# Indirect gathers of a graph kernel's second product handed out from a queue, with pauses that read fresh values

## The chip, the cores and the metric

The kernel runs on one core of one Trainium2 chip. The time is device microseconds of one execution; the number to predict is the median over runs of the changed kernel. A trace of one profiled execution shows every instruction of the engines: TensorE (PE; its weight loads are PEld), VectorE (DVE), ScalarE (ACT), GpSimd (POOL) and SyncE (SP), and the DMA queues.

## The reference

Four graph layers run on the same 4096 nodes with 128 features, each with a residual and a layer norm. `adj` is a 4096 x 4096 matrix with about two entries per thousand outside its diagonal.

```python
x = _layernorm(x + L0(x, adj))     # signed attention over adj
x = _layernorm(x + L1(x, adj))     # Chebyshev, K = 3, twice
x = _layernorm(x + L2(x, adj))     # 4-head attention over adj.T
x = _layernorm(x + L3(x, adj))     # degree-normalised mean

def cheb_conv(x, L, W, b):         # L1 applies it twice, with elu
    Tx0 = x
    out = Tx0 @ W[0]
    Tx1 = L @ x
    out = out + Tx1 @ W[1]
    for k in range(2, W.shape[0]):
        Tx2 = 2.0 * (L @ Tx1) - Tx0
        out = out + Tx2 @ W[k]
        Tx0, Tx1 = (Tx1, Tx2)
    return out + b
```

So layer 1 multiplies `adj` four times: by x (product 1 below), by t1 = adj x (product 2), by v (product 3) and by w (product 4).

## The kernel before

The nodes are cut into 8 blocks of 512 (`IB`), each block into 4 tiles of 128. A chunk is one 512 x 512 piece of `adj`, 1 MB, brought in by SyncE. `propagate` (line 723) multiplies a stationary operand by one block row of chunks, 8 chunks a block, and after each chunk calls `seen`, which carries the side work of that moment. A call of `seen` is a hook; its number counts chunks within the product.

Some blocks are not multiplied densely at all. `adj` is sparse, so VectorE finds the entries of each row (`take`, lines 1402 and 1403: the eight largest of a row and where they are), and `Lists.build` (from line 1411; its instructions all show as line 1318) makes a list of neighbours for each block. A block that is in `LAST` (0 and 1, left out of product 2) or `PAIRED` (0, 1 and 2, left out of product 3) is then computed from gathered rows: `rows_of` gathers for each tile, called a unit, 9 times 128 rows by an index list; `weigh` (lines 1557 to 1562) scales them on ScalarE and VectorE; `product` (lines 1631 to 1640 in product 2, 1688 to 1708 in product 3) sums them on TensorE. The entries of `adj` themselves are gathered by `pairs`, 36 gathers a block, and taken over by `paired` (lines 1545 to 1547, on VectorE).

Every such gather goes through `by_index` (line 1524): an indirect DMA issued by GpSimd, followed by `pause` (line 1569), a 128 x 1 multiplication on GpSimd. A pause can be given a value to read; without one it reads a constant of its own.

Four things set the order of the work. First, within products 1 to 3 a planner orders each engine's instructions by priority and its own estimates. Second, what is passed to `tc.keep_in_program_order` keeps its order on its engine; that holds for all gathers and their pauses on GpSimd. Third, `chained` ties VectorE's instructions together in the order in which the program writes them: `take`, `paired`, `build`, `weigh`, the block's t2T (line 779) and the copy of w (line 826) in products 2 and 3. Fourth, product 4 and all that follows runs in an order written out by hand, with 3 gathers a hook.

Product 2 works on blocks 2 to 7, so its hooks run from 0 to 47. After a block, `second_end` (line 781) makes hT from three products (line 786), two elu (VectorE's part is line 721), two more products (line 791) and v (ScalarE's copy, line 793), and v goes to DRAM for the gathers of product 3. Units 0 to 7 belong to the blocks 0 and 1; their gathers land in parts of hT, t1T and xT that are free at that time. The last of their products, unit 3 and unit 7, call `second_end` for the blocks 0 and 1. Which hook does what stands in `plan`: units are pulled at hooks 0, 0, 12, 13, 25, 25, 35 and 37, the pairs of block 1 are fetched at 7, those of block 2 at 26 (12 of them) and at 45 (the rest).

Product 3 works on blocks 3 to 7 (hooks 0 to 39). It weighs 12 units, at hooks 6, 9, 11, 14 and so on, and pulls unit u + 2 in the product of unit u, into three buffers. It also builds the lists of blocks 3 to 7. Product 4 is in `sparse_layers`; after it the gathers for layer 2 begin (`early`, then `gathers`, line 1846).

Of the kernel before, what the change touches and what calls it, by code (L numbers as in the profile page):

```python
# [21 lines left out]
P = 128  # L22
IB = 512
TB = IB // P
# [15 lines left out]
PAIRED = [0, 1, 2]  # L40
# [7 lines left out]
def adj_resnorm_d4(ctx: ExitStack, tc: tile.TileContext, x_in, xT_in, adj, adjT, pairs, diag_in, w0g, w0gT, a0, w1a, b1a,  # L48
# [633 lines left out]
    def network(usual):  # L682

        with ExitStack() as whole:
# [3 lines left out]
            with ExitStack() as first, ExitStack() as l1h_pool:  # L688
# [15 lines left out]
                if usual:  # L704
                    lists = Lists(whole, first, l1h_pool, own_entries)
# [44 lines left out]
                pairs = {c: lists.pairs(c) for c in PAIRED} if usual else {}  # L750

                def fetch(c, n):
                    for _ in range(n):
                        next(pairs[c], None)

                made = lists.build(0) if usual else None
                done = []
# [18 lines left out]
                v = state.tile([P, NT, F], F32, name="v")  # L776
# [4 lines left out]
                def second_end(ib, t2T):  # L781
                    blk = slice(ib * IB, (ib + 1) * IB)
                    for hh in range(HH):
                        ph = ps_mm.tile([P, IB], F32, name="pmm")
                        for k, r in enumerate((xT[:, blk], t1T[:, blk], t2T)):
                            nc.tensor.matmul(ph, W1A[:, k, hh * P:(hh + 1) * P], r, start=k == 0, stop=k == 2)
                        elu(hT[:, hh, blk], ph, B1A[:, hh:hh + 1], B1N[:, hh:hh + 1])
                    q = ps_tr.tile([P, TB, F], F32, name="ptr")
                    for k in range(TB):
                        for hh in range(HH):  # L790
                            nc.tensor.matmul(q[:, k, :], hT[:, hh, (ib * TB + k) * P:(ib * TB + k + 1) * P],
                                             w2x[:, hh, :], start=hh == 0, stop=hh == HH - 1)
                    nc.scalar.copy(v[:, ib * TB:(ib + 1) * TB, :], q)
                    done[-1] = ib
                    if usual:
                        lists.store(0, ib, v)

                second = second_product(lists, l1w, pairs, t1, t1T, xT, hT, v, done, t2_of, second_end) if usual else None

                for ib, blk, p in propagate(lambda jt: t1[:, jt, :], order=[0, 4, 1, 5, 2, 6, 3, 7], seen=second, blocks=[b for b in range(NB) if not usual or b not in LAST]):  # L800
                    t2T = l1w.tile([P, IB], F32, name="t2T")
                    r = t2_of(t2T, p, blk)
# [5 lines left out]
                w = state.tile([P, NT, F], F32, name="w", tag="yn")  # L808
# [1 line left out]

                third = None
                if usual:
                    fetch(PAIRED[-1], TB * 9)
                    lists.paired(PAIRED[-1])
                    l1s = l1h_pool.enter_context(tc.tile_pool(name="l1s", bufs=2, reuse_waits="tile"))
                    third = third_product(lists, l1s, ps_tr, ps_mm, v, w, hT, W1B, wd, h0T)
# [5 lines left out]
                for ib, blk, p in propagate(lambda jt: v[:, jt, :], beside=times_w1, seen=third, blocks=[b for b in range(NB) if not usual or b not in PAIRED]):  # L822
                    lvT = l1w.tile([P, IB], F32, name="t2T")
                    nc.scalar.copy(lvT, p)
                    q = transpose4(ps_tr, "ptr", lambda k: lvT[:, k * P:(k + 1) * P])
                    r = nc.vector.tensor_copy(w[:, ib * TB:(ib + 1) * TB, :], q)
                    if usual:
                        lists.chained(r)
                        lists.store(1, ib, w)
                    ph = ps_mm.tile([P, IB], F32, name="pmm")  # L830
                    for hh in range(HH):
                        nc.tensor.matmul(ph, wd[:, hh, :], hT[:, hh, blk], start=hh == 0, stop=hh == HH - 1)
                    nc.scalar.copy(h0T[:, blk], ph)
# [337 lines left out]
            with tc.manual_schedule(engines={mybir.EngineType.PE, mybir.EngineType.DVE, mybir.EngineType.Activation,  # L1171
# [126 lines left out]
                this, nt, _, tau2 = behind.popleft()  # L1298
# [21 lines left out]
    class Lists:  # L1320
# [3 lines left out]
        def __init__(self, whole, first, layer, own_entries):  # L1324
# [9 lines left out]
            self.at = keep.tile([P, NT - TB, NB, 8], U16, name="at")  # L1334
            self.diag = own_entries
            self.last = None
            nc.scalar.dma_start(self.diag, diag_in)
            self.source = keep.tile([P, NT, NEAR + QT], I32, name="source")
            self.value = keep.tile([P, NT, NEAR + QT], F32, name="value")
            self.where = keep.tile([P, NT, QT], I32, name="where")  # L1340
            units = len(PAIRED) * TB
# [13 lines left out]
            with tc.tile_pool(name="lists_i", bufs=1) as pool:  # L1355
                i = pool.tile([P, SLOTS], I32, name="i")
                for t, pattern, base, step in ((self.slot, [[1, SLOTS]], 0, 0), (self.place, [[0, TB], [P, QT]], 0, 1),
                                               (self.first, [[IB, NB], [0, 8]], 1, 0), (self.own, [[0, 1]], 0, 1)):
                    n = flat(t).shape[1]
# [162 lines left out]

        def by_index(self, out, of, index):
            tc.keep_in_program_order(nc.gpsimd.indirect_dma_start(out, None, of, bass.IndirectOffsetOnAxis(ap=index, axis=0)))  # L1524
            tc.keep_in_program_order(self.pause())

        def values(self, c):
            flat = adjT.rearrange("a b p k i -> (a b p k i)")[:, None]
# [76 lines left out]
    def second_product(lists, pool, pairs, t1, t1T, xT, hT, v, done, t2_of, second_end):  # L1605
        units = len(LAST) * TB
        E = NEAR + QT
        late = slice(5 * IB, 8 * IB)
        soon = slice(2 * IB, 5 * IB)
        places = [t[:, cols].rearrange("p (j f) -> p j f", f=F)  # L1610
                  for t, cols in ((hT[:, 0], late), (hT[:, 1], late), (t1T, soon), (xT, soon))]
        got = places[0:2] * 2 + places[2:4] * 2
        made, sums = {}, {}
        plan = {}

        def at(h, f, *args):
            plan.setdefault(h, []).append(lambda: f(*args))

        def fetch(c, n):
            for _ in range(n):  # L1620
                next(pairs[c], None)

        def pull(u):
            deque(lists.rows_of(u, got[u], 2), 0)

        def weigh(u):
            here = pool.tile([P, F], F32, name="here2", bufs=1)
            lists.weigh(u, t1[:, tile_of(u), :], got[u], here, got[u][:, E:E + QT, :], True)
            made[u] = here

        def product(u):
            t, k = tile_of(u), u % TB
            if k == 0:
                sums[0] = pool.tile([P, IB], F32, name="t2T")
            p = lists.psum.tile([P, P], F32, name="u")
            nc.tensor.matmul(p, made.pop(u), ident, start=True, stop=False)
            for j in range(QT):
                nc.tensor.matmul(p, got[u][:, j, :], got[u][:, E + j, :], start=False, stop=j == QT - 1)
            t2_of(sums[0][:, k * P:(k + 1) * P], p, slice(t * P, (t + 1) * P))
            if k == TB - 1:  # L1640
                second_end(PAIRED[u // TB], sums.pop(0))

        for c, h in ((1, 0), (2, 14)):
            build = lists.build(c, True)
            for n in range(3):
                at(h + 3 * n, next, build)
        at(0, pull, 0)
        at(0, pull, 1)
        at(7, fetch, 1, TB * E)
        at(8, lists.paired, 0)  # L1650
        at(26, lists.paired, 1)
        for u, h in enumerate((9, 11, 27, 30, 33, 35, 41, 44)):
            at(h, weigh, u)
            at(h + 1, product, u)
        for u, h in ((2, 12), (3, 13), (4, 25), (5, 25), (6, 35), (7, 37)):
            at(h, pull, u)
        at(26, fetch, 2, 12)
        at(45, fetch, 2, TB * E)
        hooks = [0]

        def seen(ib, n, c, a):
            h = hooks[0]
            hooks[0] += 1
            if c in FAR:
                lists.take(ib, c, a, True)
            for f in plan.pop(h, ()):
                f()
            if h == 47:
                assert not plan and not made and not sums
        return seen  # L1670
# [63 lines left out]
    def sparse_layers(enter, lists, w, h0T):  # L1734
# [4 lines left out]
        E = NEAR + QT  # L1739
        W = 3 * H + 1  # L1740
        ld = ld_of[0]
        rows = state.tile([P, NT, F + H], F32, name="rows", tag="v")
# [93 lines left out]
        got, told, wide = {}, {}, {}  # L1836
# [172 lines left out]
        with tc.manual_schedule(engines={mybir.EngineType.PE, mybir.EngineType.DVE, mybir.EngineType.Activation,  # L2009
# [22 lines left out]
            def pull():  # L2032
                for u in range(len(LAST) * TB):
                    pulled[u] = l2.tile([P, E, F + H], F32, name="got", bufs=4)
                    yield from lists.rows_of(u, pulled[u], 1)
                for c in (4, 5, 6, 7):
                    yield from lists.values(c)
# [7 lines left out]
            def product(u):  # L2045
                c, k = PAIRED[u // TB], u % TB
                if k == 0:
                    apart[c] = ps_p.tile([P, IB], F32, name="pp")
                p = apart[c][:, k * P:(k + 1) * P]
                here, into = weighed.pop(u)  # L2050
                g = pulled.pop(u)
                nc.tensor.matmul(p, here[:, 0:F], ident, start=True, stop=False)
                for j in range(QT):
                    nc.tensor.matmul(p, g[:, j, 0:F], into[:, j, :], start=False, stop=j == QT - 1)
                if k == TB - 1:
                    end = block_end(c, apart.pop(c))
                    next(end)
                    others.append(end)

            plan = {}  # L2060
            for u, h in enumerate((7, 10, 13, 16, 19, 22, 25, 28)):
                plan.setdefault(h, []).append(lambda u=u: weigh(u))
                plan.setdefault(h + 1, []).append(lambda u=u: product(u))
            pulls = pull()
            known = None
            load_spread(0)
            order = [0, 1, 3, 4, 5, 6, 2, 7]
            hook = 0
# [119 lines left out]
```

## Time and profile before

| what | value |
|---|---|
| median of 13 runs | 1638.67 us (1635.86 to 1640.21) |
| the profiled execution | 1641.54 us, its span 1639.7 us |
| mean granted TensorE clock | 0.952 |
| busy: TensorE, VectorE, GpSimd, ScalarE | 1473.6, 1139.7, 839.1, 387.4 us |
| share of the chain that ended last: PE, DVE, DMA, POOL | 46%, 28%, 8%, 7% |
| product 2, from its first to its last chunk product | 564.2 to 800.9 us |
| first chunk product of product 3, of product 4 | 804.2, 1003.1 us |
| both_ways gathers (pairs) | 108, median 974 ns |
| pauses that read the constant | 508, median 205 ns |

A row of a timeline gives start and duration in us, engine, line, operation, the tiles written and read, shapes and count; square brackets hold the idle time of the engine just before, with what ended it. Idle time of an engine that nobody waits for costs nothing, and shares over the whole span mix stages with different limits.

### The profile page before, as it was taken

The numbers are of one execution on the slowest core, as the hardware profiler recorded it, in microseconds if no ns is written. First come the engines' busy times: TensorE is split into PE (matmuls) and PEld (weight loads), VectorE is DVE, ScalarE is ACT, GpSimd is POOL, SyncE is SP. The second block draws the span as 40 slices with busy tenths as digits, with TensorE's granted clock in tenths as the row PEclk, the third lists the DMA queues.
The fourth block names the chain that finished last, engine by engine and source line by source line (L and its number), as shares of the span: only waits on it lengthen the run. The fifth ranks groups of instructions, "written<-read, shape, count | busy, mean of one in ns | idle before, by whom it ended". The sixth has DMA issues, their size and how long they took to land.

```text
span 1639.7 us, 16500 instructions
## 1 busy us (share of the span) xinstructions
PE 1473.6 (90%) x4740; PEld 711.6 (43%) x4744; DVE 1139.7 (70%) x3209; ACT 387.4 (24%) x698; POOL 839.1 (51%) x1336
## 2 busy tenths in 40 slices
PE   6899999999999999999999999999916798789885
PEld 3344444544444444444444454545413344444344
DVE  5987655788978887998699971455326756556766
ACT  5775540010000011121200000222313111122234
POOL 0000000000243088848485888888886688888841
PEclk9999999999999999999999999999966788889988
DMA  9867776479798885867587889998874577678773
GB/s 381 340 258 298 256 258 247 169 265 316 298 324 309 308 290 176 296 213 273 171 302 260 263 275 318 315 303 296 258 176 134 178 242 244 224 240 282 233 191 102
DMA packets 111199, 421.47 MB, mean 257 GB/s; under 512 B 21685, under 2 KB 48314, under 8 KB 71290
## 3 DMA queue, kind: packets, MB, share of 16 engines
q1 hardware_dynamic: 59984, 360.01, 61.4%
q0 software_dynamic: 22656, 36.17, 8.9%
q10 hardware_dynamic: 28458, 24.14, 5.1%
q8 instruction: 39, 0.64, 0.2%
q14 instruction: 62, 0.51, 0.1%
HBM read 404.39 MB, written 15.86 MB: 256 GB/s over the span
## 4 chain that ended last, share of the span: by engine, by line
PE 46%; DVE 28%; DMA 8%; POOL 7%; issue 6%; ACT 3%; ACTq 0%; DVEq 0%; POOLq 0%; SPq 0%
PE pacc L731 12%; PE pacc L424 12%; PE pp L2076 7%; DVE at L1403 5%; PE pp L1957 5%; DVE top L1402 4%; DMA got<-table,source 4%; POOL got L1846 3%; DVE gw L1882 2%; DMA chunk<-in_adjT 2%; DVE acc L1970 2%; POOL got L1524 1%; DVE here L1884 1%; DVE here L1562 1%; POOL idle L1569 1%
## 5 line engine op out<-in xcount | busy, mean ns | idle before, releaser
L1846 POOL DMA_INDIRECT got<-table,source x267 | 255.5, 957 | 64.0 <-issue 57.1
L1957 PE MATMUL pp<-chunk,xT 128*128 128x512 f32 x496 | 245.0, 636 | 1.3 <-ACT xT L1928 0.7
L731 PE MATMUL pacc<-chunk,x 128*128 128x512 f32 x512 | 223.1, 593 | 1.0 <-DMA chunk<-in_adjT 1.0
L1524 POOL DMA_INDIRECT got<-rows,source x180 | 183.7, 1021 | 67.4 <-issue 37.6
L424 PE MATMUL pacc<-chunk,hw 128*128 128x512 f32 x408 | 188.6, 607 | 0.8 <-DVE hw L467 0.7
L1360 POOL IOTA i<- 128x384 int32 (+3 forms) x4 | 0.9, 237 | 346.6 <-PE pden L412 329.2
L731 PE MATMUL pacc<-chunk,t 128*128 128x512 f32 x384 | 171.5, 597 | 0.0
L2076 PE MATMUL pp<-chunk,w 128*128 128x512 f32 x384 | 170.2, 592 | 0.0
L731 PEld LDWEIGHTS pacc<-chunk,x 128*128 128x128 f32 x512 | 95.9, 190 | 116.3 <-issue 113.7
L731 PE MATMUL pacc<-chunk,v 128*128 128x512 f32 x320 | 144.5, 597 | 0.0
L1402 DVE MAX8 top<-chunk 128x8 f32<-128x512 f32 x196 | 128.6, 678 | 14.9 <-DMA chunk<-in_adjT 14.9
L1957 PEld LDWEIGHTS pp<-chunk,xT 128*128 128x128 f32 x496 | 94.9, 204 | 91.9 <-issue 85.8
L1403 DVE FIND_INDEX8 at<-top,chunk 128x8 uint16<-128x512 f32 x196 | 133.1, 685 | 0.0
L1569 POOL TENSOR_TENSOR idle<-idle 128x1 f32<-128x1 f32 x508 | 115.7, 228 | 8.9
L1524 POOL DMA_INDIRECT both_ways<-in_pairs,both_at x108 | 106.8, 989 | 17.4 <-issue 17.0
L424 PEld LDWEIGHTS pacc<-chunk,hw 128*128 128x128 f32 x408 | 75.0, 192 | 91.9 <-issue 86.2
L731 PEld LDWEIGHTS pacc<-chunk,t 128*128 128x128 f32 x384 | 71.7, 192 | 81.8 <-issue 81.8
L396 ACT ACTIVATE junk<-chunk 128x2048 fp8e4<-128x2048 f32 x51 | 97.4, 1909 | 28.5 <-DMA chunk<-in_adjT 27.9
L2076 PEld LDWEIGHTS pp<-chunk,w 128*128 128x128 f32 x384 | 70.5, 190 | 77.3 <-issue 76.5
L330 DVE TENSOR_SCALAR pos<-chunk 128x2048 bf16<-128x2048 f32 x66 | 80.2, 1221 | 33.7 <-DMA chunk<-in_adjT 33.6
L1889 PE MATMUL u<-gw,into 128*128 128x132 f32 x192 | 33.7, 320 | 70.5 <-DVE gw L1882 70.5
L731 PEld LDWEIGHTS pacc<-chunk,v 128*128 128x128 f32 x320 | 58.3, 190 | 65.5 <-issue 65.5
(433 smaller groups left out, 2063.3 us busy)
## 6 DMA issues: line engine op xcount, KB each, us to landing
chunk<-in_adjT SPq DMA_DIRECT2D x326, 1024.0 KB
keep<-in_adjT SPq DMA_DIRECT2D x13, 1024.0 KB
spread<-spread ACTq DMA_DIRECT2D x16, 384.0 KB
got<-table,source POOLq DMA_INDIRECT x267
chunk<-in_adjT ACTq DMA_DIRECT2D x4, 1024.0 KB
got<-rows,source POOLq DMA_INDIRECT x180
table<-rows ACTq DMA_DIRECT2D x8, 264.0 KB
xT<-in_xT ACTq DMA_DIRECT2D x8, 256.0 KB
```

The lines of the kernel that those rows point to most:

```text
L330: r = nc.vector.tensor_scalar(pos, a, 0.0, None, op0=ALU.is_gt)
L396: nc.scalar.activation(junk, a, AF.Relu, scale=-1.0, accum_out=bad[:, n:n + 1], saturate=False)
L424: in_order(nc.tensor.matmul(p, hw[:, j * TB + k, :], a[:, k, :], start=first and k == 0, stop=last and k == TB - 1))
L731: nc.tensor.matmul(p, stationary(c * TB + k), a[:, k, :], start=n == 0 and k == 0, stop=n == NB - 1 and k == TB - 1)
L1402: pin(nc.vector.max(self.top[:, t, ib, :], row))
L1403: pin(nc.vector.max_index(self.at[:, t - TB, ib, :], self.top[:, t, ib, :], row))
L1524: tc.keep_in_program_order(nc.gpsimd.indirect_dma_start(out, None, of, bass.IndirectOffsetOnAxis(ap=index, axis=0)))
L1569: return nc.gpsimd.tensor_tensor(self.idle[:, 0:1], of, self.idle[:, 1:2], ALU.mult)
L1846: nc.gpsimd.indirect_dma_start(got[t][:, j, :], None, table, bass.IndirectOffsetOnAxis(ap=lists.source[:, t, j:j + 1], axis=0))
L1889: nc.tensor.matmul(so, into[:, j, :], gw[:, j, :], start=j == 0, stop=False)
L1957: nc.tensor.matmul(p, y[:, t0 + k, :], a[:, ib % (TB // n), k, :], start=k == 0, stop=k == n - 1)
L2076: nc.tensor.matmul(p, w[:, c * TB + k, :], a[:, k, :], start=n == 0 and k == 0, stop=n == NB - 1 and k == TB - 1)
```

## The change

Only units and pairs of product 2 are concerned by the queue; the pauses of all gathers that go through `by_index` are.

- `ask` puts a generator of gathers in a queue, with the hook from which it may be handed out. `feed`, called at the end of every hook of product 2, adds 3.4 to a credit, hands out one gather for each whole unit of it, in the queue's order, and keeps at most 3.4. `finish` hands out everything up to and including one generator, or everything that is left.
- The pulls and fetches of product 2 are asked for in place of being issued at once: units at hooks 2, 2, 12, 14, 25, 25, 35 and 37, pairs at 7, 26 and 45. `weigh` and `paired` call `finish` for what they need. What is left after product 2 is handed out before `paired` of block 2.
- `by_index` gives its pause `lists.fresh` to read: a column of the newest v, of the newest t2T of a unit, or of the newest w, as the program has written them so far. It starts as None and is set to None again after product 3.

```diff
-                    done[-1] = ib
                     if usual:
+                        lists.fresh = v[:, ib * TB, 0:1]
                         lists.store(0, ib, v)
...
-                    fetch(PAIRED[-1], TB * 9)
+                    lists.finish()
                     lists.paired(PAIRED[-1])
...
                         lists.chained(r)
+                        lists.fresh = w[:, ib * TB, 0:1]
                         lists.store(1, ib, w)
...
+            self.fresh = None
+            self.queue, self.credit = deque(), 0.0
...
-            tc.keep_in_program_order(self.pause())
+            tc.keep_in_program_order(self.pause(self.fresh))
+
+        def ask(self, hook, rows):
+            self.queue.append((hook, rows))
+            return rows
+
+        def feed(self, hook, rate):
+            self.credit += rate
+            while self.credit >= 1 and self.queue and self.queue[0][0] <= hook:
+                if next(self.queue[0][1], self) is self:
+                    self.queue.popleft()
+                else:
+                    self.credit -= 1
+            self.credit = min(self.credit, rate)
+
+        def finish(self, rows=None):
+            while self.queue and any(rows is None or r is rows for _, r in self.queue):
+                deque(self.queue.popleft()[1], 0)
...
-        def pull(u):
-            deque(lists.rows_of(u, got[u], 2), 0)
+        rows = [lists.rows_of(u, got[u], 2) for u in range(units)]
+
+        def some(c, n):
+            for _ in range(n):
+                if next(pairs[c], pairs) is pairs:
+                    return
+                yield
 
         def weigh(u):
+            lists.finish(rows[u])
...
             t2_of(sums[0][:, k * P:(k + 1) * P], p, slice(t * P, (t + 1) * P))
+            lists.fresh = sums[0][:, k * P:k * P + 1]
             if k == TB - 1:
                 second_end(PAIRED[u // TB], sums.pop(0))
...
-        at(0, pull, 0)
-        at(0, pull, 1)
-        at(7, fetch, 1, TB * E)
+        def known(c):
+            lists.finish(asked[c])
+            lists.paired(c)
+
+        asked = {}
+        for h, what in ((2, 0), (2, 1), (7, (1, TB * E)), (12, 2), (14, 3), (25, 4), (25, 5), (26, (2, 12)), (35, 6), (37, 7), (45, (2, TB * E))):
+            if isinstance(what, int):
+                lists.ask(h, rows[what])
+            else:
+                asked[what[0]] = lists.ask(h, some(*what))
         at(8, lists.paired, 0)
-        at(26, lists.paired, 1)
+        at(26, known, 1)
...
-        for u, h in ((2, 12), (3, 13), (4, 25), (5, 25), (6, 35), (7, 37)):
-            at(h, pull, u)
-        at(26, fetch, 2, 12)
-        at(45, fetch, 2, TB * E)
...
             for f in plan.pop(h, ()):
                 f()
+            lists.feed(h, 3.4)
...
+            lists.finish()
+            lists.fresh = None
             pulls = pull()
```

## The prediction

> **What bounds the kernel now.** I read the page first (engine shares, then the 40 slices), then a table of busy time by stage, then the order of time on GpSimd, VectorE, ScalarE and TensorE around product 2, product 3 and the start of the sparse layers. The table of stages comes first here; its columns are stretch, length, busy time of each engine with instructions in brackets, granted clock, DMA share, GB/s.
>
> ```profile
> 564.00:620.00 56.00, 55.30 (x167) 26.27 (x166) 50.98 (x135) 6.94 (x11) 39.27 (x64) 1.00 0.84 290
> 764.00:804.00 40.00, 39.52 (x126) 19.98 (x125) 24.90 (x61) 7.69 (x14) 28.40 (x47) 1.00 0.60 198
> 804.00:884.00 80.00, 74.36 (x226) 33.59 (x225) 72.58 (x264) 8.18 (x15) 48.32 (x72) 1.00 0.77 274
> 884.00:967.00 83.00, 78.23 (x267) 38.57 (x266) 77.26 (x282) 6.03 (x13) 68.73 (x106) 1.00 0.79 266
> 1003.00:1100.00 97.00, 93.54 (x286) 46.65 (x286) 38.62 (x130) 17.56 (x33) 83.50 (x147) 1.00 0.93 315
> 1201.00:1235.00 34.00, 0.40 (x8) 0.31 (x6) 6.45 (x24) 5.16 (x10) 27.84 (x44) 0.50 0.78 181
> ```
>
> Product 2 (564 to 804) keeps TensorE full. That hides what sets the end, which the last row shows: TensorE does 0.40 us in 34 us there. Who is late then is on the timelines of TensorE and GpSimd:
>
> ```profile
> 1187.87 1.26 POOL L1569 TENSOR_TENSOR idle<-rows,idle 128x1 f32<-128x1 f32 x5
> 1189.84 0.97 POOL L1524 DMA_INDIRECT got<-table_early,source  x1 [0.71 <-issue]
> 1219.42 0.97 POOL L1846 DMA_INDIRECT got<-table,source  x1 [0.15 <-issue]
> 1234.84 1.69 PE L1889 MATMUL u<-gw,into 128*128 128x132 f32 x6 [33.60 <-DVE gw L1882]
> ```
>
> GpSimd gathers with gaps of 0.15 us, and TensorE waits for the last of those gathers. Five pauses stand back to back just before: GpSimd was behind all through the first sparse product. Going back, its gaps stay below 1.2 us as far as 888.61. So GpSimd is a solid line from 888.61 to 1234, and what starts it late there, ends everything late. What starts it at 888.61 is the weighing of unit 1 on VectorE:
>
> ```profile
> 805.32 0.18 DVE L1546 COPY value<-both_ways 128x36 f32<-128x36 f32 x1
> 805.56 0.29 DVE L1318 TENSOR_SCALAR there<-top 128x256 f32<-128x256 f32 x1
> 818.21 0.16 DVE L1318 COPY base<-u 128x4 f32<-128x4 f32 x1 [1.84 <-PE u L1454]
> 884.82 0.85 DVE L1559 TENSOR_SCALAR hot<-iota,into_column,back 128x128 f32<-128x128 f32 x3
> 885.22 1.00 PE L1694 MATMUL ptr<-got,hot 128*128 128x128 f32 x6
> 888.61 0.97 POOL L1524 DMA_INDIRECT got<-rows,source  x1 [12.54 <-issue]
> ```
>
> VectorE is one chained order from `paired(2)` (805.32) through three list builds to 884.82; the only wait printed there is 1.84 us. So the path is: `paired(2)` on VectorE, 80 us of list building, product of unit 1, GpSimd's 346 us of gathers, the sparse layers.
>
> **The change, part by part.** *Queue arithmetic.* I counted `feed` by hand (3.4 a hook, what is left over capped at 3.4). All units and the pairs of block 1 are handed out before their `finish` would force them. The 24 last pairs of block 2, asked for at hook 45, come as 6, 4 and 3 at hooks 45 to 47, and 11 in `finish()` after product 2. Before, all 24 ran without a wait up to 796.1 (last line below).
>
> *What the pauses read there.* At hook 45 `product(7)` runs first and calls `second_end(1)`, so the pauses of the first 13 read v of block 1. The other 11 read v of block 7, whose `second_end` follows hook 47. These are the two ScalarE copies (first two lines), and the GpSimd rows for the pace:
>
> ```profile
> 796.66 0.59 ACT L793 COPY v<-ptr 128x512 f32<-128x512 f32 x1 [1.52 <-PE ptr L791]
> 814.74 0.59 ACT L793 COPY v<-ptr 128x512 f32<-128x512 f32 x1 [2.98 <-PE ptr L791]
> ...
> 793.76 0.97 POOL L1524 DMA_INDIRECT both_ways<-in_pairs,both_at  x1 [0.15 <-issue]
> 795.11 0.97 POOL L1524 DMA_INDIRECT both_ways<-in_pairs,both_at  x1 [0.15 <-issue]
> ```
>
> One gather with its pause takes 795.11 - 793.76 = 1.35 us. Gather 1 of the 24 runs at about 763; its pause waits until 797.25 (796.66 + 0.59), and behind it on GpSimd stand the other 23, then units 0 and 1 of product 3 and all later gathers; `paired(2)` waits for the 24. Gather 2 starts at 797.6, twelve take 16.2, so gather 14 starts at 813.8; its pause waits until 815.33. Gathers 15 to 24 start from 815.7; the last at 815.7 + 9 x 1.35 = 827.9.
>
> *Landing.* The chain shows 2.34 us from the start of a gather to its reader in one place (1229.84) and 5.08 in another (971.40). So `paired(2)` reads at 830.2 to 833.0; I take 831.5, nearer the lower end, since 1 KB is little. The Trainium skill, "DMA: Bandwidth & Descriptors", section on the anatomy of a SWDGE DMA, gives about 2.0 us fixed for each such DMA; counted from the end of the issue, that would be 830.9, which agrees.
>
> *VectorE.* L1546 moves from 805.32 to 831.5: 26.2 us later, and everything chained waits behind it: builds 3 to 7, all weighing, the copies of w. In the meantime VectorE can do only the two unchained L721 of block 7 (0.6 us each, 1.2 in all), perhaps saving the 1.84 wait too. Shift of the chained order: 23.2 to 25.0, I take 24.5. No wait between 805 and 885 takes it up, so the product of unit 1 comes at 909.7 and GpSimd's unit 4 starts at 913.1.
>
> *GpSimd at the start of product 3.* Its first gather moves from 818.67 to 829.2, 10.6 us; that lies inside the 12.54 us before 888.61 and costs nothing by itself.
>
> *Pauses in product 3.* They read v of block 7, then w of the block just ended. Only one is late beside its gather: unit 6 starts at 914.83, its first gather ends at 915.94, and it reads w of block 4,
>
> ```profile
> 914.83 1.11 POOL L1524 DMA_INDIRECT got<-rows,source  x1 [0.15 <-issue]
> ...
> 919.61 0.68 DVE L826 COPY w<-ptr 128x512 f32<-128x512 f32 x1
> ```
>
> done at 920.2. Both are 24.5 later, so the wait is about 4.3 us, and GpSimd has no slack. Unit 3 waits some 9 us for w of block 3 (872.47), but then it waits for the product of unit 1 anyway. Unit 9 (955.90, w of block 5 at 959.09) is already 4.3 late: nothing. From below the term is 0, from above 4.3 for each of units 6 and 9, 8.6.
>
> *Earlier waits in product 2.* The pairs of block 1 and units 2 and 3 end at 679.5 instead of 676; weighing of unit 2 is at 700.9. Units 4 and 5 wait for v of block 4 (about 693.3) and end at 716; they are weighed at 726.2 and 735.2. Units 6 and 7 were held by the products of 4 and 5 before, too. Cost nothing, hidden by those 10 to 20 us. A pause reads 128x1 as before: 0.20 us. The removed `done[-1] = ib` is Python alone.
>
> *What could be gained.* TensorE waits 7.8 us in all for VectorE in product 2. Its rows name t2T, hT and here, none behind a gather; gain from 0 to 7.8, I take 0, as TensorE's end of product 2 starts nothing that is late.
>
> *A rule weighed.* Gathers last 0.97 us beside VectorE's searches in product 2 (above) and 1.24 us beside the list builds (823 to 829). The Trainium skill, "SBUF — State Buffer", on the trap in which VectorE blocks a DMA, says that descriptor writing is shut out while certain VectorE instructions run. By that rule the 10 gathers from 815.7 would save 10 x 0.27 = 2.7 us, as VectorE stands still; I have counted them at the undisturbed 1.35 already.
>
> **Sum.** 24.5 + 4.3 = 28.8 us, against the profiled execution's 1641.54: 1670.3. That execution lies 2.9 above the median of 1638.67, so I say 1667.5. TensorE starts the first sparse product later as well, by some 14 to 22 us, less than GpSimd, so it doesn't add. From 1235 on the order is unchanged; a clock other than the 0.87 there by 0.01 would move TensorE's 327 busy us by 3.8.
>
> **Rivals.** (a) *Not slower.* The pauses pace gathers alongside TensorE, the 7.8 us of TensorE's waits in product 2 go, and the late `paired(2)` finds slack: 1638.7 - 7.8 = 1631. It decides if 26 us of waiting that ends elsewhere lies between 805 and 1234 on VectorE or GpSimd; I find 1.84 and about 12.5, the latter being VectorE's own lateness. Chance 0.05. (b) *VectorE is not held.* If builds come before `paired(2)` in VectorE's real order, only GpSimd's start (hidden) and the 4.3 remain: 1643. Against it: in the trace L1546 stands directly before build 3, and both are chained. Or the planner takes up half of the shift: 1653. Together 0.11. (c) *More waits in product 3.* Unit 9 also waits (4.3), and TensorE, in order, stands at a list matmul for a late VectorE, which delays w and the pauses on it by another 5: 1677. For it: TensorE waits 1.2 and 1.4 at such places now. Chance 0.14. (d) *The change does not bind*: if a pause is not held by v, all is as before, 1639; the pauses in product 1 that read t1 are held (16.55 us at 483.98), so 0.05. My forecast: 0.65.
>
> **Range and chances.** About 0.2% (3.3 us) is what can be told from no change here; the 13 runs span 1635.86 to 1640.21. The forecast's own range is 23.2 + 0 to 27.0 + 8.6 with 4 for the clock either way: 1658 to 1678. Reaching to the half-absorbed case below and (c) above gives 1652 to 1680, leaving out (a), (d) and the 1643 of (b). Faster 0.05, same 0.05, slower 0.90.
>
> **What would show it.** Right: a GpSimd pause ending near 797 after some 33 us, one near 815.4, the last both_ways gather near 828, L1546 near 831 with a wait of 16 to 18 us before it, unit 4 near 913, one wait near 944 for w, and early gathers near 1219. Wrong: L1546 before 815, builds ahead of it, or early gathers at 1190 again. I would be wrong most easily if the planner, which orders the unpinned work by its own estimates, moves block 7's end or block 1's end.

## The result, and the profile after

| | before | after |
|---|---|---|
| median | 1638.85 us (31 runs, 1635.81 to 1645.73) | 1663.47 us (7 runs, 1661.28 to 1667.92) |
| ratio, 95% interval | | 1.0153 (1.014 to 1.0166) |
| the profiled execution | 1641.54 us, span 1639.7 | 1667.97 us, span 1666.2 |
| mean granted TensorE clock in it | 0.952 | 0.941 |

The changed kernel is 24.6 us slower. Both profiled executions lie above their medians, by 2.7 and 4.5 us. Line numbers move: by_index 1524 to 1527, the pause 1569 to 1589, paired's value copy 1546 to 1566, unit products 1694 to 1725, the first sparse matmul 1889 to 1920.

The stages first, as in the prediction (stretch, length, busy time of each engine with instructions in brackets, granted clock, DMA share, GB/s), from the table of stages of the changed kernel:

```profile
764.00:804.00 40.00, 39.71 (x117) 19.21 (x116) 23.60 (x56) 8.57 (x16) 8.03 (x14) 1.00 0.65 220
804.00:884.00 80.00, 67.87 (x196) 31.02 (x195) 52.97 (x195) 5.57 (x11) 54.74 (x89) 0.94 0.70 234
1201.00:1235.00 34.00, 19.69 (x59) 9.87 (x57) 11.26 (x40) 10.20 (x19) 28.70 (x54) 0.80 0.50 127
```

In the first row GpSimd (the fifth busy time) has 8.03 us in place of 28.40: it stands still at the end of product 2. TensorE is as busy as before there (39.71 against 39.52), so it was not delayed yet. In the second row VectorE (the third) has 52.97 in place of 72.58, 19.6 us less: now VectorE stands. In the third TensorE still works on product 4, where before it was idle and waited for the gathers of layer 2. The lateness goes from GpSimd to VectorE to everything behind. The timelines of GpSimd, ScalarE and VectorE at the end of product 2, changed kernel:

```profile
760.93 0.97 POOL L1527 DMA_INDIRECT both_ways<-in_pairs,both_at  x1 [0.15 <-issue]
793.75 0.58 ACT L793 COPY v<-ptr 128x512 f32<-128x512 f32 x1 [1.53 <-PE ptr L791]
794.48 0.19 POOL L1589 TENSOR_TENSOR idle<-v,idle 128x1 f32<-128x1 f32 x1 [32.58 <-ACT v L793]
795.14 0.97 POOL L1527 DMA_INDIRECT both_ways<-in_pairs,both_at  x1 [0.47 <-issue]
808.05 0.71 DVE L721 SCALAR_TENSOR_TENSOR hT<-elu_n,elu_r 128x512 f32<-128x512 f32 x1 [1.91 <-ACT elu_n L720]
810.92 0.58 ACT L793 COPY v<-ptr 128x512 f32<-128x512 f32 x1 [2.90 <-PE ptr L791]
825.15 0.97 POOL L1527 DMA_INDIRECT both_ways<-in_pairs,both_at  x1 [0.15 <-issue]
828.21 0.20 DVE L1566 COPY value<-both_ways 128x36 f32<-128x36 f32 x1 [19.45 <-DMA both_ways<-in_pairs,both_at]
828.43 0.47 DVE L1319 TENSOR_SCALAR there<-top 128x256 f32<-128x256 f32 x1
```

Read it from top to bottom. The first of the last 24 pair gathers goes out at 760.93. Its pause waits 32.58 us for v of block 1, which ScalarE copies at 793.75. The other 23 gathers come behind it, the last at 825.15. VectorE has finished block 7 at 808.76 and waits 19.45 us for those pairs; directly behind the value copy stands the first list build. The same thing further on, timelines of TensorE and GpSimd:

```profile
905.37 0.89 PE L1725 MATMUL ptr<-got,hot 128*128 128x128 f32 x6
908.65 0.97 POOL L1527 DMA_INDIRECT got<-rows,source  x1 [2.25 <-issue]
940.32 0.19 POOL L1589 TENSOR_TENSOR idle<-w,idle 128x1 f32<-128x1 f32 x1 [4.34 <-DVE w L826]
1212.13 0.97 POOL L1527 DMA_INDIRECT got<-table_early,source  x1 [0.72 <-issue]
1258.08 1.69 PE L1920 MATMUL u<-gw,into 128*128 128x132 f32 x6 [32.90 <-DVE gw L1913]
```

The product of unit 1 comes at 905.37 (885.22 before), unit 4 at 908.65 (888.61), the pause of unit 6 waits 4.34 us for w, and the first sparse matmul comes at 1258.08 (1234.84), 23.2 us later.

Positions in two traces are best compared from a common point. I take the first gather of product 2: 575.44 in the trace of before, 574.00 in that of after. The value copy of block 2 then stands at 229.9 and 254.2, a shift of 24.3. Two later traces of kernels without the delay have it at 227.3 and 227.4, so the profiled execution of before had lost some 2.5 us inside product 2, and the shift is nearer 26.8.

### The profile page after: what moved, and what is told of

It reads as the page before. It is cut to its first block, busy times and chain, and to the rows that moved or that the text cites. A ratio compares the mean times of both kernels' runs of the same rounds, so it can differ in the third digit from the quotient of the medians.

```text
span 1666.2 us, 16489 instructions
## 1 busy us (share of the span) xinstructions
PE 1480.2 (89%) x4740; PEld 716.4 (43%) x4744; DVE 1140.8 (68%) x3209; ACT 387.1 (23%) x698; POOL 836.6 (50%) x1336
## 4 chain that ended last, share of the span: by engine, by line
PE 47%; DVE 22%; POOL 17%; issue 6%; DMA 5%; ACT 3%; ACTq 0%; DVEq 0%; POOLq 0%
PE pacc L731 15%; PE pacc L424 12%; POOL got L1877 6%; PE pp L2109 6%; PE pp L1988 4%; DMA got<-table,source 3%; POOL got L1527 3%; DVE at L1406 3%; POOL idle L1589 3%; DVE top L1405 2%; POOL value L1527 2%; POOL both_ways L1527 1%; DVE here L1915 1%; PE pden L412 1%; DVE gw L1913 1%
## 5 line engine op out<-in xcount | busy, mean ns | idle before, releaser
L731 PE MATMUL pacc<-chunk,v 128*128 128x512 f32 x320 | 149.4, 611 | 0.0
L1582 DVE SCALAR_TENSOR_TENSOR here<-got,back,here 128x128 f32<-128x128 f32 x120 | 42.3, 353 | 45.3 <-DMA got<-rows,source 42.2
```

The costliest lines, as they stand in the source:

```text
L731: nc.tensor.matmul(p, stationary(c * TB + k), a[:, k, :], start=n == 0 and k == 0, stop=n == NB - 1 and k == TB - 1)
L1582: pin(nc.vector.scalar_tensor_tensor(here, got[:, j, 0:F], self.back[:, u, j:j + 1], here, op0=ALU.mult, op1=ALU.add))
```

## Experiments

Eight kernels came to chips on which the kernel before itself takes 1782 us (the first four) or 1808 us (the next four); the last four came to chips on which it takes 1639 us. Each ratio is against the kernel before on the same chip. On the slower chips the traces agree with the others as far as product 2 (from 336 to 563 us TensorE is busy 226.87 us with the queue alone on the chip of 1782 us, 226.95 with plain last pauses on a chip of 1639 us), and then whole stretches of several engines stand still. What is said of them here rests on kernels that ran side by side, and on the waits in their traces. The prices are taken from the last four.

### Which part makes VectorE wait

*The queue alone.* All pauses read the constant again:

```diff
-            tc.keep_in_program_order(self.pause(self.fresh))
+            tc.keep_in_program_order(self.pause())
```

> The queue as in the changed kernel, but every pause reads the constant again. Theory (the pauses after the last 24 pairs hold paired(2), and with it VectorE, unit 1 of product 3, GpSimd and the end): nothing holds GpSimd any more, the 24 pairs end near 796 as before, L1546's successor near 805, time 1639, within 4 us of before. Rival Q (handing the gathers out later and in small lots is what costs): 1655 to 1663. Rival P (the planner's other order costs): 1650 or more.

*The pauses alone.* The kernel before, with the lines of the change that set `lists.fresh` and the pause that reads it; units and pairs are issued as before:

```diff
                     if usual:
+                        lists.fresh = v[:, ib * TB, 0:1]
...
-            tc.keep_in_program_order(self.pause())
+            tc.keep_in_program_order(self.pause(self.fresh))
```

> No queue, units and pairs issued at the hooks of before, but each pause reads the newest v, t2T or w as in the changed kernel. Theory: at hook 45 all 24 pairs read v of block 1, which comes near 794 to 797, so they end near 826 to 829 as in the changed kernel; time 1660 to 1666. Rival Q (the queue costs): 1639 to 1645.

*The last 24 pauses plain.* The changed kernel, where the pauses of the last 24 pairs read the constant; all others still read v, t2T and w:

```diff
-        def by_index(self, out, of, index):
+        def by_index(self, out, of, index, free=False):
...
-            tc.keep_in_program_order(self.pause(self.fresh))
+            tc.keep_in_program_order(self.pause(None if free else self.fresh))
...
-                    yield self.by_index(self.both[:, u, j, :], flat, self.both_at[:, u, j:j + 1])
+                    yield self.by_index(self.both[:, u, j, :], flat, self.both_at[:, u, j:j + 1], c == PAIRED[-1] and (u - n * TB) * (NEAR + QT) + j >= 12)
```

> The changed kernel, only the pauses after the last 24 pairs of block 2 read the constant. Theory: paired(2) is back near 805, unit 4 of product 3 near 888; what is left is the pause of unit 6 that reads w of block 4, 4.3 us: 1641 to 1645. Rival W (the pauses of product 3 are the main cost): 1655 or more. Rival P (other order): 1650 or more.

*The last 24 pairs asked for later.* The changed kernel with `(48, (2, TB * E))` in place of `(45, (2, TB * E))`, so that all of them come after product 2 and read v of block 7:

> The changed kernel with the last 24 pairs asked for at hook 48, so that all are handed out after product 2 and all pauses read v of block 7 (811.5 in place of 794.3 in the changed kernel's trace). Theory: first pause 17 us later, the 24 end near 843, paired(2) reads near 845 in place of 828.2, everything after it 14 to 17 us later again: 1676 to 1680. Rival Q or W: as the changed kernel, 1663 within 4.

| kernel, on the chip of 1782 us | median | ratio (95%) | wait of VectorE at the value copy |
|---|---|---|---|
| queue alone | 1784.14 | 1.0015 (0.9986 to 1.0044) | none |
| pauses alone | 1808.95 | 1.0119 (1.0082 to 1.0156) | 19.39 |
| last 24 pauses plain | 1741.19 | 0.9746 (0.9704 to 0.9788) | none |
| last 24 pairs later | 1789.52 | 1.0027 (0.9996 to 1.0058) | 36.15 |

VectorE's timeline of the queue alone, then GpSimd's and VectorE's of the pauses alone, then of the last 24 pairs asked for later:

```profile
871.62 0.17 DVE L1566 COPY value<-both_ways 128x36 f32<-128x36 f32 x1
```

```profile
848.38 0.19 POOL L1572 TENSOR_TENSOR idle<-v,idle 128x1 f32<-128x1 f32 x1 [38.15 <-ACT v L793]
882.06 0.18 DVE L1549 COPY value<-both_ways 128x36 f32<-128x36 f32 x1 [19.39 <-DMA both_ways<-in_pairs,both_at]
```

```profile
824.39 0.19 POOL L1589 TENSOR_TENSOR idle<-v,idle 128x1 f32<-128x1 f32 x1 [49.75 <-ACT v L793]
857.63 0.25 DVE L1566 COPY value<-both_ways 128x36 f32<-128x36 f32 x1 [36.15 <-DMA both_ways<-in_pairs,both_at]
```

So it is the pause, not the queue, that makes VectorE wait: pauses without the queue have the wait of 19.4 us, the queue without the pauses has none. The two differ by 24.8 us on this chip. With all 24 pairs behind v of block 7, the wait is 36.15, and this kernel is 48.3 us longer than the one with plain pauses.

The times were a miss in their level, though. Plain last pauses were to give the time of before and gave 2.5% less; the later pairs were to give 2.3% more and gave 0.3%. On this chip something else seems to gain in the kernels that have both the queue and the other pauses of product 2; that is not shown to be the reason. The last section comes back to it.

### Where the wait is passed on

Four kernels on the chip of 1808 us. The plain last pauses again:

> The changed kernel, but the pauses of the last 24 pairs read the constant (the pauses of all other gathers of product 2 and of product 3 still read v and w). It is run a second time because the first four runs fell on a chip on which the kernel before itself takes 1782 us and whole stretches of product 2 stand still; here the positions in the trace count as much as the time. Theory (the 33 us that GpSimd stands at the first of these pauses set the end): VectorE's first value copy for block 2 has no wait for a DMA before it, the early gathers follow the start of unit 4 by the same 301 us, and the time is that of before plus 0 to 4.3 us: 1639 to 1643 where before is 1639 (ratio 1.000 to 1.003). Rival (the queue and the many other pauses cost it): 1655 to 1663, ratio 1.010 to 1.015.

*The reader moved.* The changed kernel keeps its pauses and its late pairs, but the VectorE instructions that read them (`paired` of block 2) come at hook 20 of product 3:

```diff
                     lists.finish()
-                    lists.paired(PAIRED[-1])
...
+        plan.setdefault(20, []).append(lambda: lists.paired(PAIRED[-1]))
```

> The changed kernel with one step moved: the four VectorE instructions that read the pairs of block 2 are issued at hook 20 of product 3, behind the list builds, instead of at the end of product 2. The pauses, the queue and GpSimd's late end stay as they are. Theory (the loss passes through VectorE's chained order, which stands 19 us at this read): no wait of 19 us before the builds, the product of unit 1 about 20 us earlier, and 1639 to 1645 (ratio 1.000 to 1.004). Rival (GpSimd's own lateness is what is passed on, as its first gather of product 3 moves from 818.7 to 826.5): 1655 to 1664, ratio 1.010 to 1.015.

*The pauses of product 3 plain:*

```diff
                     lists.finish()
+                    lists.fresh = None
                     lists.paired(PAIRED[-1])
...
-                        lists.fresh = w[:, ib * TB, 0:1]
```

> The changed kernel, but the pauses in product 3 read the constant instead of w. Theory (of the 24.8 us, 4.3 are the pause of unit 6, which waits for w of block 4): 1657 to 1661 where before is 1639 (ratio 1.011 to 1.013), and the gathers of units 7 to 11 come 4 us earlier. Rival (TensorE or VectorE are as late there anyway and GpSimd's 4 us are lost again before the early gathers): 1663 to 1665, ratio 1.0145 to 1.016.

*Weighing earlier.* The kernel before, with less list building ahead of the weighing of units 0 and 1. The list of a block is built in three steps, one at each hook that the condition lets through. With `h < 3` only hook 4 drops out, so it is one step fewer, and not two list builds as the expectation below says; the hooks of the weighing stay where they are:

```diff
-            if h < 5 or h % 2:
+            if h < 3 or h % 2:
                 next(build, None)
```

> The kernel before with one condition changed: in product 3 the weighing of a unit is called at every odd hook from 3 on instead of from 5 on (h < 3 instead of h < 5 are the hooks that a list build takes in any case), so the weighing of units 0 and 1 comes before two of the list builds. Theory (VectorE's list builds ahead of the weighing of unit 1 set the start of GpSimd's solid stretch, which waits 12.5 us there): unit 4 starts up to 12 us earlier and the time is 1627 to 1634 (ratio 0.993 to 0.997). Rival (the later builds then hold the weighing of the next units, or TensorE, or GpSimd is not the bound by itself): 1637 to 1645, ratio 0.999 to 1.004.

| kernel, on the chip of 1808 us | median | ratio (95%) | start of unit 4 |
|---|---|---|---|
| last 24 pauses plain | 1770.69 | 0.9806 (0.9742 to 0.987) | 925.6 |
| reader moved | 1761.38 | 0.9727 (0.967 to 0.9783) | 906.8 |
| pauses of product 3 plain | 1787.96 | 0.9887 (0.9853 to 0.9922) | 954.9 |
| weighing earlier | 1791.15 | 0.9918 (0.9887 to 0.9948) | 951.3 |

None of the four ratios lies in the range that was expected of it; on this chip the level tells little. The waits tell more. Of the first three, only the one with plain pauses in product 3 keeps the hold and its reader in place, and only it has the wait. GpSimd's and VectorE's timelines of it:

```profile
817.24 0.19 POOL L1589 TENSOR_TENSOR idle<-v,idle 128x1 f32<-128x1 f32 x1 [32.57 <-ACT v L793]
850.97 0.18 DVE L1566 COPY value<-both_ways 128x36 f32<-128x36 f32 x1 [19.43 <-DMA both_ways<-in_pairs,both_at]
```

It takes 17.3 us more than the kernel with plain last pauses, and 26.6 more than the one whose reader is moved. Both point to the path through VectorE. What the pauses of product 3 cost by themselves, this run does not tell, as the changed kernel was not beside it.

### The price, on chips of 1639 us

The changed kernel and the one with plain last pauses, side by side:

> The changed kernel itself, run beside the variant that only frees the last 24 pauses of product 2, so that the two stand on one chip. Two of the chips used so far run the kernel before in 1782 and 1808 us with long standstills in product 2, where the first chip needs 1639. Theory: on any chip VectorE's first value copy for block 2 waits some 19 us for the pairs, and the time is longer than that of the variant beside it, by 22 to 30 us. On a chip of 1639 the ratio to before is then 1.014 to 1.017; on a slow one, where the kernel with plain pauses for product 3 took 0.989 of before, it is 0.985 to 1.005. Rival (the standstill is only a symptom there, and the end is set by the disturbed gathers): no difference between the two beyond 8 us.

> The changed kernel with plain pauses behind the last 24 pairs alone, beside the changed kernel on one chip. Theory: no wait of VectorE for the pairs before the list builds, unit 4 of product 3 starts 20 us or more before that of the changed kernel, and the whole is 22 to 30 us shorter: 1.000 to 1.003 of before on a chip of 1639, 0.972 to 0.984 on a slow one. Rival: within 8 us of the changed kernel.

Measured: 1666.47 us, ratio 1.0167 (1.0148 to 1.0185), and 1644.19 us, ratio 1.0039 (1.0025 to 1.0052). The 24 pauses are worth 22.3 us of the 27.4 that the change cost on this chip. In the trace of the changed kernel VectorE waits as in the first one:

```profile
828.14 0.18 DVE L1566 COPY value<-both_ways 128x36 f32<-128x36 f32 x1 [19.34 <-DMA both_ways<-in_pairs,both_at]
```

With the last 24 pauses plain, the table of stages and the timelines of GpSimd and VectorE read:

```profile
804.00:884.00 80.00, 74.45 (x234) 34.42 (x233) 72.51 (x264) 5.85 (x11) 49.66 (x72) 1.00 0.75 261
...
791.59 0.97 POOL L1527 DMA_INDIRECT both_ways<-in_pairs,both_at  x1 [0.15 <-issue]
800.88 0.17 DVE L1566 COPY value<-both_ways 128x36 f32<-128x36 f32 x1
884.15 0.97 POOL L1527 DMA_INDIRECT got<-rows,source  x1 [2.24 <-issue]
915.81 0.19 POOL L1589 TENSOR_TENSOR idle<-w,idle 128x1 f32<-128x1 f32 x1 [4.34 <-DVE w L826]
1010.87 0.97 POOL L1527 DMA_INDIRECT got<-rows,source  x1 [2.76 <-issue]
```

VectorE is back at 72.51 us in the stage (72.58 in the kernel before), the value copy waits for nothing, and unit 4 starts at 884.15. All other pauses of product 2 and the queue are still there: they wait 2.57, 1.20 and 11.48 us for v, and the value copy stands 227.4 us after product 2's first gather, where a kernel without queue and pauses has 227.3 (the weighing earlier, below, which is the kernel before up to there). So they cost nothing in product 2. The 5.1 us that remain arise behind unit 4: unit 4 itself is level with the kernel before (310.6 us after product 2's first gather, 313.2 - 2.5 = 310.7 there, with the 2.5 us of its slow product 2 taken off), but the last w is stored 431.8 us after it, in place of 427.7 - 2.5 = 425.2. The pause of unit 6, 4.34 us, stands between the two; no run shows that it alone is the cause.

The reader moved, on a chip of 1639 us (the expectation speaks of four instructions; `paired` has three, and two of them read the pairs):

> The changed kernel with the four VectorE instructions that read the pairs of block 2 moved to hook 20 of product 3; the 33 us pause and GpSimd's late end of the pairs stay. It is run again because the changed kernel and its variant with the last pauses plain have now been seen side by side on a chip of 1639 (1666.5 and 1644.2). Theory (the loss passes through VectorE alone; GpSimd's first gather at 826.5 instead of 818.7 is hidden): unit 4 of product 3 starts at 884 to 891, as with the plain pauses (884.2), the pause of unit 6 waits about 4 us, and the time is 1640 to 1647, ratio 1.001 to 1.005. Rival (half or more of the loss passes through GpSimd): unit 4 after 895, 1652 or more, ratio over 1.008. On a slow chip: 0.968 to 0.980, as before.

Measured: 1642.19 us, ratio 1.0025 (1.0013 to 1.0036). Its timelines of GpSimd and VectorE:

```profile
793.23 0.19 POOL L1588 TENSOR_TENSOR idle<-v,idle 128x1 f32<-128x1 f32 x1 [32.58 <-ACT v L793]
828.84 0.97 POOL L1526 DMA_INDIRECT got<-rows,source  x1 [0.15 <-issue]
884.37 0.97 POOL L1526 DMA_INDIRECT got<-rows,source  x1 [2.25 <-issue]
935.46 0.17 DVE L1565 COPY value<-both_ways 128x36 f32<-128x36 f32 x1
```

This separates the two ways out of the hold. GpSimd waits the same 32.58 us and is as late as ever: its first gather of product 3 is at 828.84, 10 us later than in the kernel before (818.67). But VectorE builds lists meanwhile and reads the pairs at 935.46, so unit 4 starts at 884.37, 310.2 us after product 2's first gather, where the changed kernel beside the plain last pauses has 334.1. The 24 us between them are gone. GpSimd's own lateness costs nothing; that VectorE stood in front of a few small instructions cost nearly all of it.

*Weighing earlier,* on that chip:

> The kernel before with h < 3 instead of h < 5 in product 3, run again: on the slow chip the time from VectorE's first value copy for block 2 to the start of unit 4 was 72.9 us, where the kernel before has 83.3 on the first chip. Theory (VectorE's work ahead of the weighing of unit 1 sets GpSimd's solid stretch): unit 4 starts about 10 us earlier, near 878, and the time is 1627 to 1634, ratio 0.993 to 0.997. Rival (the work put off holds the weighing of units 5 to 8 or w instead, so that GpSimd gets a new wait): unit 4 near 878 all the same, but the early gathers at 1186 to 1192 and the time 1636 to 1643, ratio 0.998 to 1.003.

Measured: 1636.92 us, ratio 0.9989 (0.9976 to 1.0002): no difference can be told. The time is the rival's, and GpSimd does get a new wait, though the early gathers come at 1181.90 and not at 1186 to 1192. ScalarE's and GpSimd's timelines show why:

```profile
872.81 0.97 POOL L1524 DMA_INDIRECT got<-rows,source  x1 [4.50 <-issue]
997.95 0.37 ACTq L1565 DMA_DIRECT2D rows<-w  x1
1002.67 0.97 POOL L1524 DMA_INDIRECT got<-rows,source  x1 [5.64 <-PE pp L2076]
```

And the same place in the kernel before:

```profile
1003.11 0.37 ACTq L1565 DMA_DIRECT2D rows<-w  x1
1009.18 0.97 POOL L1524 DMA_INDIRECT got<-rows,source  x1 [0.15 <-issue]
```

Unit 4 starts 299.2 us after product 2's first gather, in place of 313.2; some 2.5 of the difference are the slow product 2 in the profiled execution of before, so the gain there is about 11 us. Up to the last gather ahead of product 4 GpSimd then needs 124.2 us in place of 120.4, so some 7.6 of the 11 are left there. Then the first gather of product 4 reads rows of w, and w of the last block is stored at 997.95. GpSimd waits 5.64 us, and goes on 4.72 us after the store was issued. (The row names TensorE's first chunk product of product 4, which starts with the store, at 997.97; that the landing of the store is what ends the wait is read from the program. Either way it is the last w that GpSimd waits for.) In the kernel before it follows the store by 6.07 us without a wait. So TensorE's product 3, with the store behind it, was only about 6.07 - 4.72 = 1.4 us behind GpSimd as the bound (in two other traces that wait for the store it is 5.5 us, which would leave half a microsecond), and little more than that could be won on GpSimd's side: 2.1 us came out, within what the interval leaves open. The 0.8% won on the chip of 1808 us is not found here.

No kernel here beats the kernel before on a chip of 1639 us by more than can be told.

## Why the prediction was right

It said 1667.5 us, with 1652 to 1680; 1663.47 was measured, and 1666.47 on another chip. The steps, one by one:

- *Queue arithmetic:* 24 pairs, 32.6 us of hold at the first. Right: the pause that ends at 794.48 stands where 797.25 was said; of the 2.8 us between them, 1.4 are the earlier start of product 2. The gathers behind it kept the pace of 1.35 us.
- *What the pauses read:* a second wait, for v of block 7, was to come at gather 14. It did not come: v was copied at 810.92, and the pause of gather 14 was at 812.7. With that and the earlier start the last gather is at 825.15 in place of 827.9. The margin had been half a microsecond, and nothing hung on it.
- *Landing:* 3.06 us from the last gather to its reader (828.21 - 825.15); 3.6 was taken. The rows had bounded it by 2.34 and 5.08.
- *VectorE:* the value copy was to shift by 26.2 and the work chained behind it by 24.5. Beside the kernel with plain last pauses, the copy shifts by 254.2 - 227.4 = 26.8 and unit 4 by 334.65 - 310.63 = 24.0 (positions after product 2's first gather, here and below). Right, and by moving the reader it is shown that this is the path.
- *GpSimd at the start of product 3:* hidden. Shown by the same run.
- *Earlier waits in product 2,* and a gain of 0 there: right to 0.1 us by the position of the value copy.
- *Pauses in product 3:* 4.3 at unit 6, none at unit 9. The wait is there with 4.34 us, and unit 3 waits 8.73 without harm, as said. Two kernels whose hold does no harm but which keep this pause take 5.1 and 3.2 us more than the kernel before, so the size fits; a run that takes this pause alone away on a chip of 1639 us was not made, so this term is not shown by itself.
- *The sum* said that nothing takes up any of the 24.5 after 884 us. That is the step that was off by a little: the early gathers, said near 1219, came at 1212.13. From unit 4 to the first gather of product 4 the shift shrinks from 24.0 to 21.7 us (459.1 - 437.4), because there the undelayed kernel waits 2.76 us for the store of w, which the delayed one does not. At the first sparse matmul it is 19.9 (684.1 - 664.2). The last stretch, from there to the end, was longer by some 5 us in both profiled executions of the changed kernel (408.1 and 408.2 us, 402.8 with plain last pauses, 404.9 in the kernel before); I have no cause for that. How much of it stands in the 22.3 between the medians is open, as the spans of these executions differ by 25.7 and 26.7. In the range, the upper shift of 27.0 does not come out of the 23.2 to 25.0 worked out above it; with 24.0 measured, nothing hung on that.
- *The first view* called GpSimd a solid line from 888.61 to 1234 and drew the path through it alone. It is solid, but TensorE's product 3 runs level with it up to 1009. That did not show in the forecast, since the change delayed both by much the same; it would have made a forecast of a gain wrong by about 10 us, as it made my theory for the earlier weighing wrong. That it did no harm here was luck.

Of the rivals, *VectorE is not held* (1643) describes exactly the kernel whose reader is moved, which took 1642.19.

## What to carry to other kernels

A wait that is put on one engine costs what stands behind its late product, in order, on the next engine: look for the first reader of what comes late, and for what is queued behind that reader. Moving a few short instructions of 0.2 us behind work that was ready brought the cost from 1.67% down to 0.25%, with the 32.6 us wait left as it was. And before an engine without gaps is called the bound, ask at each place where it hands over to other data (here the store of w) how far behind the next bound is; here it was 1.4 us, and of the 11 us that unit 4 gained, 2.1 came out.

## What was not expected of the hardware

On two chips the kernel before takes 140 to 170 us more than on the others, and the variants traced there lose their time from product 2 on. In the 227 us before it (336 to 563) TensorE is busy 226.87 us with the queue alone on the chip of 1782 us. Then it falls to about half in the two stretches below, although GpSimd gathers at the same pace. The table of stages of the queue alone on that chip, and of the kernel before on the first chip:

```profile
600.00:620.00 20.00, 9.71 (x19) 4.41 (x20) 10.02 (x27) 4.96 (x7) 17.45 (x31) 0.74 0.22 57
620.00:640.00 20.00, 10.20 (x32) 5.66 (x31) 3.72 (x9) 0.00 (x0) 17.48 (x30) 0.67 0.30 102
```

```profile
600.00:620.00 20.00, 19.58 (x70) 10.52 (x69) 19.37 (x51) 6.35 (x10) 17.58 (x30) 1.00 0.80 280
620.00:640.00 20.00, 17.01 (x39) 7.34 (x38) 18.06 (x65) 0.00 (x0) 17.47 (x30) 0.96 0.50 163
```

GpSimd is busy 17.5 of 20 us in all four rows, while in the first two together TensorE does a little over half as much as in the last two, VectorE and the DMA queues little more than a third. Timeline of the queue alone at the end of that run of gathers ("remote" is a releaser that the profile cannot name):

```profile
646.80 0.97 POOL L1527 DMA_INDIRECT both_ways<-in_pairs,both_at  x1 [0.15 <-issue]
650.97 0.58 ACT L793 COPY v<-ptr 128x512 f32<-128x512 f32 x1 [33.59 <-remote]
651.20 0.29 DVE L779 SCALAR_TENSOR_TENSOR t2T<-u,xT 128x128 f32<-128x128 f32 x1 [27.38 <-remote]
651.35 0.97 POOL L1527 DMA_INDIRECT hT<-rows,source  x1 [3.35 <-remote]
```

ScalarE and VectorE, which had waited 33.59 and 27.38 us, go on within 0.4 us of each other, 4.2 us after the start of the last gather of an unbroken run. The like happens at 841.69 to ScalarE's copy of v, after 25.69 us and 2.0 us after the start of the last pair gather of product 2. So on these chips other engines seem to be held while GpSimd gathers without a break, and a program that holds GpSimd back now and then may be faster there: the changed kernel with its last 24 pauses plain took 0.975 and 0.981 of the kernel before, where it took 1.004 on a chip of 1639 us. But the queue alone took 1.0015 and the pauses alone 1.0119 of it, and the earlier weighing, which holds nothing back, 0.9918, so this is not shown. What holds them (the updates of semaphores, the loading of instructions, something else) none of these runs tells, and the changed kernel itself was not timed on such a chip, nor was the kernel before traced there.
